# Turning diagonal blocks by DMA instead of by TensorE in a neighbour-skipping stage

## The chip, the cores and the metric

The kernel runs on one core of a Trainium2 chip. The metric is device time in microseconds: the median over runs of one execution of the whole kernel. Engines are named as in the profile: PE (TensorE, with PEld for its weight loads), DVE (VectorE), ACT (ScalarE), POOL (GpSimd) and SP (SyncE, which here issues DMAs only). A single profiled execution gives the trace that is read below.

## The reference, cut to what matters

There are 16 graphs of 1024 nodes with 128 features. Layer 0 is a gated graph network: four times, messages are gathered over the adjacency matrix and a GRU cell updates the node states. Layer 1 is a three-layer graph convolution on a thinned ("dilated") adjacency matrix. The thinning goes row by row over each matrix, and each row's removals also clear the matching column, so later rows see what earlier ones removed:

```python
row = jnp.take(carry, n, axis=0)
num = jnp.sum(row.astype(jnp.int32))
sf = jnp.where(num > T_DIL, (num + K_DIL - 1) // K_DIL, 1)
rank = jnp.cumsum(row.astype(jnp.int32))
rm = row & (rank % sf == 0)          # dropped where the mask and num > 1 allow
carry = carry.at[n].set(row & ~rm)
carry = carry.at[:, n].set(carry[:, n] & ~rm)
```

Layer 0 uses the full adjacency, and both layers end in a residual sum and a layer norm.

## The kernel before, in words

The first stage runs layer 0 (class `Gated`) and the thinning (class `FixPoint`) side by side. Everything after it (class `Sage`) is layer 1. The order of instructions on every engine, SP included, is the order in which the program writes them: the stage is scheduled by hand.

`Gated` keeps two graphs under way. A layer of one graph is, for PE, two passes of the message matmuls (L1092, a high and a low part) and then, for two halves, the gate matmuls (L1104) with turns of the other graph's state between them (L1037). Gate results lie in six PSUM banks that are used in rotation. DVE reads two of them per half (L1116, L1118), and PE can take a bank again only when its reader is done. POOL updates the state (L1123 to L1125) and issues the loads of the adjacency rows (h_a) and features (h_x).

`FixPoint` works through 32 blocks. A block is 128 rows (number k of 8) of four graphs (G = 4). It is written as a generator, `steps`; `Gated` advances it by one `yield` at each of its `aside` calls, about two layers to a block. A block holds four tiles f_a of 128 x 1024 bf16, which POOL's DMAs load (L687) about one block ahead. Its work: TensorE turns the diagonal 128 x 128 block of each f_a into PSUM tile f_pd (L770); DVE multiplies it with the untransposed one (L777), which tells which pairs of new rows are joined both ways, and POOL keeps the part above the diagonal (L778). DVE drops what earlier blocks removed (`keep`, L729) and takes running sums along the rows (`count`, L737). Then come three rounds of a fixed-point iteration on the diagonal block. The scan of `count` has a second operand that its second operation bypasses; it was the first column of the turned block's PSUM tile, broadcast.

The finished block's rows are made at the start of the next block (class `Block`): four times f_u on ACT (L910, L913), f_w (L864) and f_nr (L866) on DVE; SP stores f_nr (L867) and turns its next diagonal strip by DMA into f_rt (`read_last`, L723). Older strips of f_rt come back from DRAM, again turned by DMA (`read_back`, L716), in the middle of a block. Both kinds are DMA transposes on SP's queue.

A third job crosses the two: `load_test` (L994) loads 128 rows of adjacency into h_test from SP, and `check` (L1982) has DVE look whether all are 0 or 1. A load is written at the end of one layer and its check at the start of the next one:

```python
if n == 9 and s == 0:
    self.load_test(b0 // 2 * L0 + l)
if n == 1 and s == 1 and not checked:
    self.check(b0 // 2 * L0 + l)
```

There is one such pair per block. The tile has one buffer, so a load waits for the check before it.

Of the kernel before, what the change touches and what calls it, by code (L numbers as in the profile page):

```python
# [8 lines left out]
F32 = mybir.dt.float32  # L9
BF = mybir.dt.bfloat16  # L10
# [11 lines left out]
P = 128  # L22
B = 16
N = 1024
# [31 lines left out]
class Dilate:  # L56
# [15 lines left out]
    def __init__(self, ctx, tc, cst, adj, not_r):  # L72
        self.tc, self.nc, self.cst, self.adj, self.not_r = tc, tc.nc, cst, adj, not_r
        nc = self.nc
        pool = lambda name, **k: ctx.enter_context(tc.tile_pool(name=name, **k))
        self.one = pool("d_one", bufs=1)
        self.two = pool("d_two", bufs=2)
        self.small = pool("d_small", bufs=3)
        self.dram = pool("d_dram", bufs=1, space=DRAM)
        self.ps = pool("d_ps", bufs=1, space=PSUM)  # L80

        self.removed = [self.dram.tile([N, N], BF, name=f"rt{b}") for b in range(B)]

        self.coef = self.one.tile([B, ROW], F32, name="coef")  # L90
        nc.vector.memset(self.coef, 1.0)
        nc.vector.memset(self.coef[:, TAIL + 1:TAIL + 2], -1.0)
        nc.vector.memset(self.coef[:, TAIL + 2:TAIL + 3], -0.5)
        nc.vector.memset(self.coef[:, TAIL + 5:TAIL + 6], 2.0)
        self.stage = self.one.tile([P, B, ROW], BF, name="stage")
        for i, v in ((1, -8.5), (2, 1.0), (3, MAGIC), (4, -MAGIC), (5, 0.0)):
            nc.vector.memset(self.stage[:, :, TAIL + i:TAIL + i + 1], v)
        self.counts = self.one.tile([P, B, NB], F32, name="counts")
        self.free = {}
# [531 lines left out]
class FixPoint:  # L631
# [17 lines left out]
    G = 4  # L649
    LOTS = 8  # L650

    def __init__(self, ctx, tc, cst, adj, not_r, bad):
        self.tc, self.nc, self.cst, self.adj, self.not_r, self.bad = tc, tc.nc, cst, adj, not_r, bad
        nc, G = self.nc, self.G
        pool = lambda name, **k: ctx.enter_context(tc.tile_pool(name=name, **k))
        self.one = pool("f_one", bufs=1)
        self.two = pool("f_two", bufs=1)
        self.rows = pool("f_rows", bufs=self.LOTS)
        self.wide = pool("f_wide", bufs=3)
        self.rts = pool("f_rts", bufs=4)  # L660
        self.small = pool("f_small", bufs=2)
        self.ps = pool("f_ps", bufs=1, space=PSUM)

        tri = self.one.tile([P, P], F32, name="f_tri32")
        nc.vector.memset(tri, 1.0)
        nc.gpsimd.affine_select(tri, tri, pattern=[[1, P]], compare_op=ALU.is_ge, fill=0.0,
                                base=0, channel_multiplier=-1)
        self.tri = self.one.tile([P, P], BF, name="f_tri")
        nc.vector.tensor_copy(self.tri, tri)
        self.first = self.one.tile([P, NB, B], F32, name="f_first")  # L670
        nc.vector.tensor_scalar(self.first, cst["mask"], 0.0, -8192.0, op0=ALU.is_equal, op1=ALU.mult)


        self.tr = self.ps.tile([P, NB, P], BF, name="f_tr")
        self.sm = self.tr[:, NB - 1, :].bitcast(F32)[:, :12 * G].rearrange("p (a r g) -> p a r g", a=4, r=3)
        self.todo = [(k, b0) for b0 in range(0, B, G) for k in range(NB)]
        self.loaded = {}
        self.left = {}

    def load(self, c):  # L680

# [26 lines left out]
    def read_back(self, i, g):  # L708
# [5 lines left out]
        if k > 1:  # L714
            old = slice(0, (k - 1) * P)
            self.nc.sync.dma_start(rt[:, old], self.not_r[b0 + g, old, k * P:k * P + P], transpose=True)  # L716

    def read_last(self, i, g, nr):

        k = self.todo[i][0] + 1  # L720
        if k < NB:
            cols = slice((k - 1) * P, k * P)
            self.nc.sync.dma_start(self.left[i + 1, g][:, cols], nr[:, k * P:k * P + P], transpose=True)  # L723
# [5 lines left out]
            self.nc.vector.scalar_tensor_tensor(a[:, :k * P], rt[:, :k * P], 0.0, a[:, :k * P],  # L729
                                                op0=ALU.is_ge, op1=ALU.mult)  # L730

    def count(self, i, g, a, rank, other):
        nc = self.nc
        k, b0 = self.todo[i]
        out, start = rank[:, g, :], self.first[:, k, b0 + g:b0 + g + 1]

        nc.vector.tensor_tensor_scan(out, a, other[:, 0, 0:1].to_broadcast([P, N]), start,  # L737
                                     op0=ALU.add, op1=ALU.bypass)

    def steps(self):  # L740

        nc, G = self.nc, self.G
        for c in range(G):
            self.load(c)
        old = None
        for i, (k, b0) in enumerate(self.todo):
            diag = slice(k * P, k * P + P)

            yield
            if old:  # L750
                old.settle()
                old.wide_u(0)
            yield
            if old:
                old.wide_u(1)
                old.rows(0)
            yield
            if old:
                old.wide_u(2)
                old.rows(1)  # L760
            yield
            if old:
                old.rows(2)
                old.wide_u(3)
                old.rows(3)
            a = [self.loaded.pop((i, g)) for g in range(G)]
            pt = self.ps.tile([P, G, P], F32, name="f_pd")
            turned = pt.rearrange("p g n -> p (g n)").bitcast(BF)[:, :G * P].rearrange("p (g n) -> p g n", g=G)
            for g in range(G):
                nc.tensor.transpose(turned[:, g, :], a[g][:, diag], self.cst["ident_b"])  # L770
            yield
            if old:
                old.last_u()

            both = self.small.tile([P, G, P], BF, name="f_both")
            for g in range(G):
                nc.vector.tensor_mul(both[:, g, :], a[g][:, diag], turned[:, g, :])  # L777
            nc.gpsimd.affine_select(both, both, pattern=[[0, G], [1, P]], compare_op=ALU.is_gt, fill=0.0,  # L778
                                    base=0, channel_multiplier=-1)
            yield  # L780
            rank = self.two.tile([P, G, N], F16, name="f_rank")
            self.keep(i, 0, a[0])
            self.count(i, 0, a[0], rank, pt)
            yield
            yield
            self.keep(i, 1, a[1])
            yield
            self.count(i, 1, a[1], rank, pt)
            if i == 0:

                for c in range(G, self.LOTS):
                    self.load(c)
            yield
            yield
            yield
            self.keep(i, 2, a[2])
            self.count(i, 2, a[2], rank, pt)
            yield
            for g in range(G):
                self.read_back(i + 1, g)  # L800
            yield
            self.keep(i, 3, a[3])
            self.count(i, 3, a[3], rank, pt)

            num = self.sm[:, 0, 0, :]
            nc.vector.tensor_scalar(num, rank[:, :, N - 1], 1.0, None, op0=ALU.mult)
            q = self.params(num, 0)
            u = self.diag_u(rank[:, :, diag], q)
            if old:
                old.check()  # L810
                for g in range(G):
                    self.load(G * (i - 1) + g + self.LOTS)
            yield
            x = self.removed(u, q, both)
            yield
            yield
            pd, num = self.less(x, rank, 1)
            rd = self.small.tile([P, G, P], F16, name="f_rd")
            q = self.params(num, 1, lambda: nc.vector.tensor_sub(rd, rank[:, :, diag], pd))
            u = self.diag_u(rd, q)  # L820
            yield
            x = self.removed(u, q, both)
            yield
            old = self.Block(self, i, a, rank, both, x)
            yield
        yield
        old.settle()
        for n in range(4):
            old.wide_u(n)
            if n < 3:  # L830
                yield
            old.rows(n)
        yield
        old.last_u()
        yield
        old.check()
# [1231 lines left out]
```

## Time and profile before

| | |
|---|---|
| median of 3 runs | 2207.2 us (2204.59 to 2207.37) |
| profiled execution, its own time | 2207.94 us |
| its span, first to last instruction | 2206.2 us |
| busy: PE, DVE, ACT, POOL | 2099.8, 1836.0, 1327.2, 1233.9 us |
| transposes that go, L770 | 128, first at 33.5, last at 1224.0 us |
| scans, L737 | 128, 2345 ns each |
| DMA transposes on SP already there | 112 (L723) and 96 (L716) |
| h_test loads, L994 | 32, first issued at 1.3, last at 1231.5 us |

Layer 0 and the thinning fill the time from about 34 to 1260 us; loading and preparing of weights comes before, layer 1 after. A line of the timeline begins with start and length in microseconds, then engine ("q": of its sequencer), line, operation, output<-inputs, shape and count. A line of busy time per stretch begins with the stretch and its length; then follow busy time (and instructions) of PE, PEld, DVE, ACT and POOL, the granted PE clock, the share of the DMA engines that was busy, and GB/s. Of a DMA instruction, the length is the issue, not the transfer.

### The profile page before, as it was taken

How to read it: one execution, taken by the hardware profiler on the slowest of the kernel's cores; microseconds unless marked ns; L12 is line 12 of the kernel's file. 1: busy time of each engine (PE TensorE's matmuls, PEld its weight loads, DVE VectorE, ACT ScalarE, POOL GpSimd, SP SyncE). 2: the span in 40 equal slices, each digit the busy share in tenths (PEclk: the TensorE clock that was granted, in tenths of full speed). 3: DMA queues.
4: the chain of work that ended last, by engine and by line, in shares of the span. 5: the costliest groups of instructions: out<-in, count | busy, mean ns of one | idle time of the engine just before them, and what ended most of it. 6: DMA issues, size and time to landing. Idle time of an engine off the chain costs nothing. (4 is left out here: it accounts for less than half of the span.)

```text
span 2206.2 us, 32924 instructions
## 1 busy us (share of the span) xinstructions
PE 2099.8 (95%) x10217; PEld 1441.5 (65%) x10217; DVE 1836.0 (83%) x4213; ACT 1327.2 (60%) x3238; POOL 1233.9 (56%) x1218
## 2 busy tenths in 40 slices
PE   6999999999999999999999979999999899999987
PEld 4666556666666665666655657777777678887865
DVE  4898998889998889989889978888888666766877
ACT  3657466565656666465575656666666355555756
POOL 4458558567476475585575457777777255540002
PEclk9999999999999999999999989999999999999989
DMA  8247446366364394472584178888887577764404
GB/s 254 76 107 244 90 115 223 85 179 184 84 202 129 80 256 110 91 241 78 126 237 101 52 263 309 304 306 306 305 305 259 210 249 248 248 225 171 139 30 143
DMA packets 233853, 406.13 MB, mean 184 GB/s; under 512 B 79042, under 2 KB 100196, under 8 KB 233668
## 3 DMA queue, kind: packets, MB, share of 16 engines
q1 hardware_dynamic: 187844, 284.37, 39.4%
q0 software_dynamic: 41472, 117.46, 19.8%
q10 hardware_dynamic: 4352, 2.11, 0.4%
q8 instruction: 83, 1.36, 0.2%
q14 instruction: 102, 0.84, 0.1%
HBM read 313.48 MB, written 109.25 MB: 192 GB/s over the span
## 5 line engine op out<-in xcount | busy, mean ns | idle before, releaser
L1104 PE MATMUL h_g<-h_h,h_wh 128*128 128x512 f32 x768 | 396.1, 597 | 3.3 <-DVE h_r L1116 3.3
L1104 PE MATMUL h_g<-h_ms,h_wi 128*128 128x512 f32 x768 | 392.2, 592 | 0.0
L1123 POOL TENSOR_TENSOR h_zh<-h_r,h_h 128x512 f32<-128x512 f32 x126 | 174.2, 1382 | 257.2 <-ACT h_r L1119 254.0
L737 DVE TENSOR_TENSOR_SCAN f_rank<-f_a,f_first,f_pd 128x1024 f16<-128x1024 bf16 x128 | 299.4, 2345 | 4.2
L1092 PE MATMUL h_g<-h_a,h_hi 128*128 128x512 f32 x1024 | 278.7, 413 | 1.0 <-DMA h_a<-in_adj_dram 0.9
L1503 POOL CAST p_b<-p_at 128x512 uint8<-128x512 f32 x256 | 219.8, 881 | 84.7 <-DVE p_at L1495 52.7
L1104 PEld LDWEIGHTS h_g<-h_ms,h_wi 128*128 128x128 f32 x768 | 145.5, 190 | 184.3 <-issue 168.9
L1092 PE MATMUL h_g<-h_a,h_lo 128*128 128x512 f32 x1024 | 261.8, 392 | 0.0
L1092 PEld LDWEIGHTS h_g<-h_a,h_hi 128*128 128x128 f32 x1024 | 190.1, 188 | 61.7 <-issue 22.2
L1396 ACT ACTIVATE s_junk<-s_o 128x128 bf16<-128x128 f32 x384 | 114.0, 298 | 175.2 <-DVE s_o L1389 164.6
L1092 PEld LDWEIGHTS h_g<-h_a,h_lo 128*128 128x128 f32 x1024 | 189.8, 188 | 38.6 <-DVE h_lo L1030 0.4
L1104 PEld LDWEIGHTS h_g<-h_h,h_wh 128*128 128x128 f32 x768 | 133.3, 190 | 100.3 <-issue 72.7
L1125 POOL TENSOR_TENSOR h_h<-h_h,h_zh 128x512 f32<-128x512 f32 x126 | 179.9, 1428 | 9.9
L1119 ACT ACTIVATE h_r<-h_r,h_bi 128x512 f32<-128x512 f32 x128 | 92.4, 722 | 149.2 <-DVE h_r L1118 149.2
L1124 POOL TENSOR_TENSOR h_zh<-h_z,h_zh 128x512 f32<-128x512 f32 x126 | 162.1, 1287 | 9.9
L1095 ACT COPY h_ms<-h_g 128x512 f32<-128x512 f32 x128 | 73.8, 577 | 150.8 <-PE h_g L1092 150.6
L910 ACT ACTIVATE f_u<-f_rank,f_q 128x128 f16<-128x128 f16 (+7 forms) x128 | 110.6, 867 | 70.2 <-DVE f_rank L850 70.2
L1771 PE MATMUL q_ob<-s_wxp,q_xt 128*128 128x256 f32 x512 | 125.7, 390 | 0.3
L1982 DVE SCALAR_TENSOR_TENSOR p_junk<-p_a 128x1024 bf16<-128x1024 f32 x96 | 125.7, 1309 | 0.0
L1495 DVE SCALAR_TENSOR_TENSOR p_at<-p_nr,p_u 128x128 fp32r<-128x128 bf16 (+1 forms) x192 | 102.5, 543 | 19.4 <-ACT p_at L1487 12.6
L887 ACT ACTIVATE f_pd<-f_rank,f_q 128x128 f32<-128x128 f16 x128 | 59.1, 462 | 96.5 <-DVE f_q L701 93.4
L1413 POOL TENSOR_TENSOR q_rl<-s_r,q_rh 128x512 fp32r<-128x512 f32 x32 | 41.2, 1288 | 128.8 <-ACT q_rh L1412 105.8
(256 smaller groups left out, 4770.7 us busy)
## 6 DMA issues: line engine op xcount, KB each, us to landing
h_a<-in_adj_dram POOLq DMA_DIRECT2D x128, 512.0 KB, 9.2
p_a<-in_adj_dram SPq DMA_DIRECT2D x96, 512.0 KB
f_a<-in_adj_dram POOLq DMA_DIRECT2D x128, 256.0 KB, 6.5
e_nr<-f_nr SPq DMA_DIRECT2D x128, 256.0 KB
p_nr<-e_nr SPq DMA_DIRECT2D x32, 1024.0 KB
h_test<-in_adj_dram SPq DMA_DIRECT2D x32, 512.0 KB
s_at<-p_b SPq DMA_DIRECT2D x32, 512.0 KB
s_ag<-s_ag SPq DMA_DIRECT2D x64, 256.0 KB
```

The source lines that it names most:

```text
L737: nc.vector.tensor_tensor_scan(out, a, other[:, 0, 0:1].to_broadcast([P, N]), start, op0=ALU.add, op1=ALU.bypass)
L910: nc.scalar.activation(u[:, :n1], rank[:, g, :n1], AF.Abs, bias=q[:, 1, g:g + 1], scale=q[:, 0, g:g + 1])
L1092: nc.tensor.matmul(pm[f], part[:, j, :], st.adj[j][:, half[f]], start=(j == 0 and n == 0), stop=(j == NB - 1 and n == 1))
L1104: nc.tensor.matmul(pg, lhs, rhs, start=(i == 0), stop=(i == len(mm) - 1))
L1123: aid.tensor_tensor(d, r, h, ALU.subtract)
L1124: aid.tensor_tensor(d, z, d, ALU.mult)
L1125: aid.tensor_tensor(h, h, d, ALU.add)
L1396: self.nc.scalar.activation(junk, o[:, i, :], AF.Square, accum_out=ss[:, i:i + 1])
L1495: self.nc.vector.scalar_tensor_tensor(g["at"][:, j, c0:c0 + low], v[:, j, c0:c0 + low], 0.0, pu[:, :low], op0=ALU.is_lt, op1=ALU.is_lt)
L1503: self.nc.gpsimd.tensor_copy(g["b", f][:, j, :], g["at"][:, j, f * HF:(f + 1) * HF].bitcast(F32))
L1771: nc.tensor.matmul(pb[:, i], g["xt"][:, f, blk], self.wxp, start=(i % 2 == 0), stop=False)
L1982: nc.vector.scalar_tensor_tensor(junk, a, 0.0, a, op0=ALU.is_gt, op1=ALU.not_equal, accum_out=bad[:, c:c + 1])
```

## The change

The diagonal blocks of new rows are no longer turned by PE. A new function, `read_own`, issues one DMA transpose per graph from the f_a tile in SBUF into a new SBUF tile f_own. It is called for block 0 after its loads, and for block i + 1 at the end of block i. DVE's multiplication reads f_own. The scan's bypassed operand becomes a column of another PSUM tile (f_tr) that is set to zero once.

```diff
         self.sm = self.tr[:, NB - 1, :].bitcast(F32)[:, :12 * G].rearrange("p (a r g) -> p a r g", a=4, r=3)
+        self.none = self.sm[:, 1, 0, 0:1]
+        nc.vector.memset(self.none, 0.0)
...
+    def read_own(self, i):
+
+        if i >= len(self.todo):
+            return
+        k = self.todo[i][0]
+        t = self.own[i] = self.two.tile([P, self.G, P], BF, name="f_own")
+        for g in range(self.G):
+            self.nc.sync.dma_start(t[:, g, :], self.loaded[i, g][:, k * P:k * P + P], transpose=True)
...
-        nc.vector.tensor_tensor_scan(out, a, other[:, 0, 0:1].to_broadcast([P, N]), start,
+        nc.vector.tensor_tensor_scan(out, a, self.none.to_broadcast([P, N]), start,
                                      op0=ALU.add, op1=ALU.bypass)
...
         for c in range(G):
             self.load(c)
+        self.read_own(0)
...
-            pt = self.ps.tile([P, G, P], F32, name="f_pd")
-            turned = pt.rearrange("p g n -> p (g n)").bitcast(BF)[:, :G * P].rearrange("p (g n) -> p g n", g=G)
-            for g in range(G):
-                nc.tensor.transpose(turned[:, g, :], a[g][:, diag], self.cst["ident_b"])
+            turned = self.own.pop(i)
...
             x = self.removed(u, q, both)
             yield
+            self.read_own(i + 1)
             old = self.Block(self, i, a, rank, both, x)
             yield
```

More of the change, by code (lines that the diff above doesn't have):

```diff
@@ L675, in __init__ @@
         self.sm = self.tr[:, NB - 1, :].bitcast(F32)[:, :12 * G].rearrange("p (a r g) -> p a r g", a=4, r=3)
+        self.none = self.sm[:, 1, 0, 0:1]
+        nc.vector.memset(self.none, 0.0)
         self.todo = [(k, b0) for b0 in range(0, B, G) for k in range(NB)]
         self.loaded = {}
-        self.left = {}
+        self.left, self.own = {}, {}
     def load(self, c):
@@ L730, in keep, with count @@
                                                 op0=ALU.is_ge, op1=ALU.mult)
-    def count(self, i, g, a, rank, other):
+    def count(self, i, g, a, rank):
         nc = self.nc
@@ L782, in steps @@
             self.keep(i, 0, a[0])
-            self.count(i, 0, a[0], rank, pt)
+            self.count(i, 0, a[0], rank)
             yield
@@ L787, in steps @@
             yield
-            self.count(i, 1, a[1], rank, pt)
+            self.count(i, 1, a[1], rank)
             if i == 0:
@@ L796, in steps @@
             self.keep(i, 2, a[2])
-            self.count(i, 2, a[2], rank, pt)
+            self.count(i, 2, a[2], rank)
             yield
@@ L802, in steps @@
             self.keep(i, 3, a[3])
-            self.count(i, 3, a[3], rank, pt)
+            self.count(i, 3, a[3], rank)
             num = self.sm[:, 0, 0, :]
```

## The prediction

> **What bounds the kernel now.** I read the page, then busy time per stretch, then TensorE's own order, then what stands on SP's queue. The change lies in the first stage, from 34 to 1260 us; the busy time of that one stretch is
>
> ```profile
> 34.00:1260.00 1226.00, 1216.27 (x4548) 743.07 (x4548) 1091.48 (x2261) 746.80 (x1392) 756.78 (x732) 1.00 0.52 142
> ```
>
> PE is busy 1216 of 1226 us, DVE 1091 (89%). The ends of matmuls are modelled, so I checked PE's starts against the smallest pitch of each kind: they run like clockwork: beside a fixed 0.4 us where L1092 follows L1104, I find some 14 us of stalls in the stage. PE sets the end; DVE has 11% to spare but is tied closely to it. The timeline of PE around one group of the transposes that go:
>
> ```profile
> 679.29 1.99 PE L1092 MATMUL h_g<-h_a,h_lo 128*128 128x512 f32 x8
> 681.12 0.40 PE L770 MATMUL f_pd<-ident_b,f_a 128*128 128x128 bf16 x4
> 681.35 1.08 PE L1104 MATMUL h_g<-h_h,h_wh 128*128 128x512 f32 x2
> ...
> 688.71 0.60 PE L1037 MATMUL h_g<-ident,h_h 128*128 128x128 f32 x4
> 689.15 1.02 PE L1104 MATMUL h_g<-h_h,h_wh 128*128 128x512 f32 x2
> ```
>
> Four transposes hold PE from 681.12 to 681.35. Next the timeline of SP (columns: start, length):
>
> ```profile
> 642.07 3.70 SPq L867 DMA_DIRECT2D e_nr<-f_nr  x4
> 645.87 0.61 SPq L994 DMA_DIRECT2D h_test<-in_adj_dram  x1
> 682.52 0.33 SPq L867 DMA_DIRECT2D e_nr<-f_nr  x1
> 682.91 1.11 SPq L723 DMA_TRANSPOSE f_rt<-f_nr  x1
> ```
>
> SP issues in order and is idle for most of a block, so h_test, which DVE checks at 678.16, is issued at 645.87, far ahead of need. Then DVE from that check on:
>
> ```profile
> 678.16 1.22 DVE L1982 SCALAR_TENSOR_TENSOR h_junk<-h_test 128x1024 bf16<-128x1024 f32 x1
> 679.30 0.08 DVE L1982 DVE_READ_ACCUMULATOR h_junk<-h_test 128x1 f32 x1
> 679.45 1.37 DVE L864 TENSOR_SCALAR f_w<-f_u,f_q 128x1024 bf16<-128x1024 f16 x1
> 680.85 1.65 DVE L866 TENSOR_TENSOR f_nr<-f_w,f_a 128x1024 bf16<-128x1024 bf16 x1
> 682.42 1.49 DVE L864 TENSOR_SCALAR f_w<-f_u,f_q 128x1024 bf16<-128x1024 f16 x1
> 683.94 0.69 DVE L866 TENSOR_TENSOR f_nr<-f_w,f_a 128x1024 bf16<-128x1024 bf16 x1
> ...
> 686.80 0.60 DVE L777 TENSOR_TENSOR f_both<-f_a,f_pd 128x128 bf16<-128x128 bf16 x4
> 687.33 0.74 DVE L1116 SCALAR_TENSOR_TENSOR h_r<-h_g,h_bh,h_r 128x512 f32<-128x512 f32 x1
> ```
>
> There is no gap from the check to L1116, whose end (688.07) frees a bank that PE takes at 689.15: 1.08 us of slack. Last, the four f_a loads of the next block, issued by POOL from 666.38 to 668.67 (the tile view of f_a in that window):
>
> ```profile
> DMA to landing us min/median/max: 8.2/9.3/9.7
> ```
>
> The last lands at 668.67 + 9.7 = 678.3, after the check has begun.
>
> **What the Trainium skill says.** "VectorE: DVE Perf Modes", The three transpose paths: 390 ns for a 128x128 bf16 transpose on TensorE, 1309 ns by DMA. Here the pitch on PE is far less, 56 to 60 ns, and SP is held 1107 ns by each transpose of this shape (L723); the data of one issued at 603.44 had moved by 604.86, 1.4 us. "SBUF — State Buffer", Who interferes with whom: DVE and GpSimd share a port pair, and whichever comes second blocks. The trace agrees: L864 takes 0.48 us alone and 1.37 or 1.49 while POOL runs L1123 to L1125 (679.10 to 683.6). "DMA: Bandwidth & Descriptors", Queues, rings and completion order: each DMA engine takes the queues in turn. The trace shows transfers of several queues at once at 10 to 26 us.
>
> **The change part by part.**
>
> PE transposes. From the last L1092 before the group to the L1104 after it is 0.464 us; without a group it is 0.228. So 0.236 us per group. The first group lies in the start, 31 in the stage: 7.3 us. In seven blocks (below) PE will wait for DVE anyway and the saving only lengthens that wait: 24 x 0.236 = 5.7 us gained.
>
> DVE's L777 reads SBUF instead of PSUM: 213 ns each, 0.53 us per four. Not shown by the trace: no gain at worst, half (0.27 us) at best; taken as 0.1. Hidden, since DVE isn't the bound, except in the seven blocks, where it is below a microsecond in all.
>
> The scan's operand stays an f32 column in PSUM; 2345 ns each as before. Its memset comes once, before anything waits for DVE. Nothing for both. POOL's f_a loads get one more wait, on transposes of a block earlier: nothing, unless those were a block late.
>
> 128 new DMA transposes on SP: 4.4 us of SP per block, 142 us in all, where SP idles some 20 us per block. Each moves 32 KB as some 123 packets of 256 B that take 2.7 us of one DMA engine, 0.17 us of all 16. They land before L777 wants them: the last is issued at about 678.4 and L777 stands at 686.80. The transfers are hidden. Their place on SP is not.
>
> **What stands behind them.** In the built order of the changed program each block has on SP: four read-backs, the four new transposes of the next block, h_test, then stores and read_last. So h_test cannot be issued before the next block's four f_a tiles have landed and been turned. Before, it waited for neither. DVE waits for h_test at L1982, and behind that stand four f_w/f_nr pairs, L777 and L1116, for which PE waits.
>
> How late is it? Last f_a landing (L), against the check (C), in the block in each four where POOL issues f_a behind h_x and h_a of a new graph: L 212.82, 368.39, 522.99, 678.34, 833.12, 990.46, 1144.26; C 211.20, 367.88, 521.81, 678.16, 831.90, 989.30, 1143.11. L-C sums to 7.0 us over seven. To each I add 0.5 (three earlier transposes share saturated DMA engines with f_a), 1.2 (the fourth transpose on SP, 1.11 and its issue) and 3.6 (from h_test's issue to its data and semaphore: an undisturbed one, issued at 609.91, is through at 613.23, 3.3 us, plus a little for e_sum, issued at 678.48). DVE's wait is then 7.0 + 7 x 5.3 = 44.1 us over seven, 6.3 each.
>
> How much reaches PE? While DVE waits, POOL finishes its three operations, so DVE afterwards runs at its undisturbed lengths: 1.29 + 4 x 1.12 + 0.53 + 0.74 = 7.0 us from check to the end of L1116, taken as 7.1. In the old trace PE takes the bank 10.98 us after the check (10.96 to 10.99 in all seven). Cover: 3.88 us each. PE loses 44.1 - 7 x 3.88 = 16.9 us, 2.4 a time.
>
> In the other 25 blocks f_a lands early (in the block checked at 638.63 by 628.57): h_test arrives 1.5 to 5 us ahead of the check, nearest in the first block and where read-backs delayed it already (old landing 1099.5 against a check at 1103.16). Nothing, but thin; and they have some cover behind.
>
> Start. h_test was the second DMA, issued at 1.27, and 512 KB moved until 4.6 us while the weights were being loaded. It now comes after the start. The weights get what it used: 0.5 MB at the 266 GB/s of that stretch is 1.9 us. The last weights landed at about 28 and PE's work runs from there to 33.7 without another long wait, so I take 2 us gained (0 to 2.5). The first four own transposes wait for weights too, until some 28, and are needed at 34: hidden.
>
> Sum against the profiled execution (span 2206.2, time 2207.94, so 1.7 around it): 2206.2 - 5.7 - 2.0 + 16.9 = 2215.4 span, 2217.1 time. The median of the runs is 0.7 below that execution: 2216.4, so 2216.5.
>
> **The rivals.**
> 1. The wait does not reach PE: faster. The place is DVE's L1982; the price is the 3.88 us of cover, and the sign turns when DVE's wait falls below 3.88 + (5.7 + 2.0)/7 = 5.0 us each. If it stays under 3.88, all of 7.3 + 2 is kept: 2207.2 - 9.3 = 2198. For it: f_a could land earlier, once the old h_test no longer competes with the loads. Against: L alone is past C in all seven, and 1.2 + 3.3 follow in series.
> 2. The cover fails: POOL and DVE collide again later, ACT's f_u comes late, or read-backs make other blocks late too. With only the 0.8 us of bank slack (1.08 in the block shown), PE loses 44.1 - 5.6 = 38.5: 2207.2 - 7.7 + 38.5 = 2238. For it: thin margins elsewhere. Against: POOL's three operations depend on nothing behind the check.
> 3. It cancels: waits at the low end (3.3 instead of 3.6, no 0.5) give 44.1 - 5.6 - 27.2 = 11.3; with the gains 2207.2 - 9.3 + 11.3 = 2209, which a measurement can't tell from no change.
>
> **How the numbers follow.** A difference under about 0.2% (4.4 us) is not told from none here. Forecast case 0.62 (own range 2208 to 2226, 0.11 of it under 2211.6), rival 1 0.10, rival 2 0.18, rival 3 0.10. Faster 0.10, same 0.21, slower 0.69. The range runs from the edge of rival 1 to most of rival 2: 2203 to 2235.
>
> **What would show it.** L770 gone from PE; L1037 to L1104 waits for DVE L1116 of 2 to 3 us at seven places some 155 us apart; DVE idle before L1982 on the h_test DMA, about 44 us in all, in just those seven; L994 issued about 1.2 us after the last f_a lands; L864 and L866 undisturbed after it; PE's first L1092 about 2 us earlier. I am wrong if L1982 shows no idle time, if many other blocks wait too, or if the start does not move.

## The result, and the profile after

The changed kernel takes 2217.59 us (median of 5 runs, 2216.59 to 2218.07), the kernel before 2204.59 beside it (2201.55 to 2207.37): the ratio is 1.0057, with an interval of 1.0042 to 1.0071. It is about 0.6% slower, by 13.0 us. The profiled execution of it has a span of 2215.8 us and a time of 2217.59. Of the 9.6 us between the two profiled spans, the start took 0.9 more (first message matmul at 34.61 instead of 33.73), the first stage 14.9 more (the distance from there to the start of the last gate matmul is 1254.77 us instead of 1239.87), and layer 1 6.2 less.

The stretch from 34 to 1260 us no longer holds the same work, since the first stage now ends at 1290 us and ended at 1274. So here is the whole first stage of each, from the first message matmul to the last gate matmul, the kernel before first:

```profile
33.73:1274.20 1240.47, 1230.74 (x4598) 751.14 (x4596) 1104.21 (x2283) 758.54 (x1413) 762.27 (x736) 1.00 0.52 143
34.61:1289.97 1255.36, 1229.92 (x4473) 750.53 (x4472) 1088.57 (x2285) 758.13 (x1413) 758.57 (x735) 0.99 0.55 143
```

PE is busy 1229.9 us where it was 1230.7: it lost the transposes, but some of its matmuls take longer, as is seen below. Its idle time went from 9.7 to 25.4 us. DVE is busy 15.6 us less. The tile view of h_test tells where DVE idles:

```profile
L1004 SPq DMA_DIRECT2D h_test<-in_adj_dram x32: 571/578/1562, 48.0 to 1247.3; - x32
...
its engine sat idle before it (us, times) until:
  DMA h_test<-in_adj_dram: 33.5, 7
```

Seven waits, at the seven blocks that were named, of 3.3 to 6.7 us. The one that was shown of the kernel before is a typical one. First SP's timeline of the changed kernel, then DVE's, then PE's:

```profile
649.21 3.71 SPq L877 DMA_DIRECT2D e_nr<-f_nr  x4
681.08 5.49 SPq L727 DMA_TRANSPOSE f_own<-f_a  x4
686.62 0.58 SPq L1004 DMA_DIRECT2D h_test<-in_adj_dram  x1
```

```profile
690.58 1.23 DVE L1992 SCALAR_TENSOR_TENSOR h_junk<-h_test 128x1024 bf16<-128x1024 f32 x1 [5.47 <-DMA h_test<-in_adj_dram]
691.73 0.08 DVE L1992 DVE_READ_ACCUMULATOR h_junk<-h_test 128x1 f32 x1
691.73 0.48 DVE L874 TENSOR_SCALAR f_w<-f_u,f_q 128x1024 bf16<-128x1024 f16 x1
692.25 0.69 DVE L876 TENSOR_TENSOR f_nr<-f_w,f_a 128x1024 bf16<-128x1024 bf16 x1
...
696.23 0.62 DVE L786 TENSOR_TENSOR f_both<-f_a,f_own 128x128 bf16<-128x128 bf16 x4
696.77 0.74 DVE L1126 SCALAR_TENSOR_TENSOR h_r<-h_g,h_bh,h_r 128x512 f32<-128x512 f32 x1
```

```profile
695.29 0.60 PE L1047 MATMUL h_g<-ident,h_h 128*128 128x128 f32 x4
697.57 1.13 PE L1114 MATMUL h_g<-h_h,h_wh 128*128 128x512 f32 x2 [1.68 <-DVE h_r L1126]
```

h_test goes out at 686.62, where it went out at 645.87, and DVE idles 5.47 us for it. L874 and L876 then run at 0.48 and 0.69 us, undisturbed. From the check to the end of L1126 it is 6.93 us, and only 1.68 us of the 5.47 reach PE. The page has these waits on the costliest group of the kernel (columns after the bar: busy, mean ns, idle before it and its releaser). First before, then after:

```profile
L1104 PE MATMUL h_g<-h_h,h_wh 128*128 128x512 f32 x768 | 396.1, 597 | 3.3 <-DVE h_r L1116 3.3
L1114 PE MATMUL h_g<-h_h,h_wh 128*128 128x512 f32 x768 | 398.4, 600 | 10.8 <-DVE h_r L1126 10.8
```

So much was foreseen. Two more groups of PE idle longer, and these were not. First the kernel before, then the changed one (groups of the whole execution):

```profile
L1037 PE MATMUL h_g<-ident,h_h 128*128 128x128 f32 x512 | 77.3, 274 | 9.2 <-DVE h_h L1125 4.9 <-ACT h_r L1113 4.3
L902 PE MATMUL f_pd<-f_tri,f_x 128*128 128x128 bf16 x256 | 25.0, 220 | 1.1 <-DVE f_x L894 1.1
```

```profile
L1047 PE MATMUL h_g<-ident,h_h 128*128 128x128 f32 x512 | 77.7, 275 | 12.0 <-ACT h_r L1123 7.2 <-DVE h_h L1135 4.9
L912 PE MATMUL f_pd<-f_tri,f_x 128*128 128x128 bf16 x256 | 25.0, 220 | 7.2 <-DVE f_x L904 7.2
```

L1047 (L1037 before) waits longer for ACT, 7.2 instead of 4.3 us. L912 (L902 before) waits for DVE's f_x at four places of the stage. Before, PE idled 0.3 us at each; now 2.2 us at three of them and 0.6 at the fourth. This is PE at the first:

```profile
203.20 0.38 PE L912 MATMUL f_pd<-f_tri,f_x 128*128 128x128 bf16 x4 [2.21 <-DVE f_x L904]
203.42 0.61 PE L1047 MATMUL h_g<-ident,h_h 128*128 128x128 f32 x4
203.86 1.55 PE L1114 MATMUL h_g<-h_h,h_wh 128*128 128x512 f32 x2
205.21 1.91 PE L1114 MATMUL h_g<-h_ms,h_wi 128*128 128x512 f32 x2
```

Two gate matmuls that take 1.02 us elsewhere take 1.91 after the stall. From here on, a stall before L912 is counted from start to start beyond the usual 0.43 us: 0.4 us at each place before, now 2.37, 2.40, 2.40 and 0.71. Where does the delay in DVE's f_x come from? The waits of DVE name one more transfer (columns: total, times, longest); before, the second line was 7.4 us, 4 times, 2.3 at most:

```profile
DVE h_junk L1992 <- DMA h_test<-in_adj_dram: 33.5, 7, 6.7
...
DVE f_a L740 <- DMA f_rt<-f_nr: 10.9, 6, 3.5
```

### The profile page after: what moved, and what is told of

Same layout as the page of the kernel before. It is cut to its first block, busy times and chain, and to the rows that moved or that the text cites. A ratio compares the mean times of both kernels' runs of the same rounds, so it can differ in the third digit from the quotient of the medians.

```text
span 2215.8 us, 33030 instructions
## 1 busy us (share of the span) xinstructions
PE 2095.8 (95%) x10089; PEld 1437.7 (65%) x10089; DVE 1820.6 (82%) x4214; ACT 1326.3 (60%) x3238; POOL 1229.3 (55%) x1218
## 5 line engine op out<-in xcount | busy, mean ns | idle before, releaser
L748 DVE TENSOR_TENSOR_SCAN f_rank<-f_a,f_first,f_tr 128x1024 f16<-128x1024 bf16 x128 | 299.4, 2345 | 4.3
L787 POOL TENSOR_SCALAR_AFFINE_SELECT f_both<-f_both 128x512 bf16<-128x512 bf16 x32 | 20.5, 639 | 189.5 <-DVE f_both L786 189.5
```

Of the source, the lines that this page charges most:

```text
L748: nc.vector.tensor_tensor_scan(out, a, self.none.to_broadcast([P, N]), start, op0=ALU.add, op1=ALU.bypass)
```

## The experiments

Theory: SP's order is what costs. The own transposes wait for f_a, h_test stands behind them, DVE waits for h_test and PE for DVE. Rivals: the own transposes cost as transfers or as time of SP wherever they stand; or the loss comes from the late f_rt strips alone. In all there are two switches, PE's transposes (kept or gone) and the own transposes (none, ahead of h_test, or behind it), and the runs fill all six cells.

**h_test ahead of the own transposes.** Against the changed kernel:

```diff
             first = n == 7 and before not in (0, L0)
+            if n == 9 and s == 0:
+                self.load_test(b0 // 2 * L0 + l)
             if not first and n not in ("rest", 8):
                 next(steps, None)
             for job in jobs.get(n, ()):
                 job()
-            if n == 9 and s == 0:
-                self.load_test(b0 // 2 * L0 + l)
```

> The changed kernel with two things on SP's queue swapped: each block's h_test load is written ahead of the four own transposes instead of behind them; everything else is the same. In the trace of the changed kernel I count two kinds of new PE stalls in the first stage: behind DVE's seven waits for h_test (33.5 us on DVE, about 10.9 us on PE with the slow matmuls that follow one of them), and at about 203, 517, 831 and 1147 us, where DVE waits for an f_rt strip turned from f_nr (about 6.2 us on PE above what was there before, and 5.0 us of matmuls at double pitch behind three of them). Theory (head of line, for both: h_test at the same time crowds the queue of the strips only if it is late): the seven waits go to 0, and the time falls by 10.9 us at least, to 2206.7, and to 2195.5 if the second kind goes too. Rival (the second kind comes from the own transposes themselves): the second kind stays, 2206 to 2207. Rival (the transfers of the own transposes slow everything whatever their order): within 4 us of the changed kernel, 2214 to 2218.

Measured: 2201.76 us, ratio to the kernel before 0.9974 (0.9962 to 0.9987). SP's timeline, at the place shown above:

```profile
641.04 3.71 SPq L877 DMA_DIRECT2D e_nr<-f_nr  x4
644.80 0.73 SPq L1004 DMA_DIRECT2D h_test<-in_adj_dram  x1
673.10 5.79 SPq L727 DMA_TRANSPOSE f_own<-f_a  x4
```

No wait for h_test is left. The own transposes are all there and still stand ahead of the stores and strips of the next block. The same instructions in another order turn a loss of 0.6% into a gain of 0.26%. The rival that blames the transfers falls. The second kind of stall did not go: one of the four places still stalls 2.40 us, and the others 0.71 or 0.72 instead of 0.4.

**The own transposes added to the kernel before.** PE still turns the blocks and nobody reads f_own:

```diff
...
+        self.read_own(0)
         old = None
...
+            self.read_own(i + 1)
             old = self.Block(self, i, a, rank, both, x)
```

> The kernel before with the 128 own transposes added at the changed kernel's place on SP, into a tile that nobody reads; PE still turns the blocks and DVE and the scan read those. It prices the transposes on SP's queue alone. Theory: all that was lost comes from there: the seven waits for h_test and the late strips, 10.9 + 11.2 = 22.1 us, and 0.9 in the start: 2204.6 + 23 = 2227.6, or about 3 us less since layer 1 ran that much shorter in the changed kernel. Rival (the loss needs f_own as DVE's operand, or the missing PE transposes): 2204 to 2212.

Measured: 2220.45 us, 1.0055 (1.0041 to 1.0069). The view of h_test:

```profile
  DMA h_test<-in_adj_dram: 42.7, 8
```

The whole loss is there without the change's other half, but not the 22 to 23 us that I had expected: the late strips hardly came along (one stall of 2.07 us before the same matmul, three of 0.4), and the waits for h_test are longer than in the first trace of the changed kernel. It looks as if the two were coupled: what holds up DVE ahead of the check leaves less of a wait for h_test. The ledger below returns to it.

**The same, behind h_test.**

```diff
             first = n == 7 and before not in (0, L0)
+            if n == 9 and s == 0:
+                self.load_test(b0 // 2 * L0 + l)
...
-            if n == 9 and s == 0:
-                self.load_test(b0 // 2 * L0 + l)
```

> The kernel before with the 128 own transposes added into a tile that nobody reads, as in the run of 2220.5 us, but written behind the h_test load of their block instead of ahead of it. PE still turns the blocks. Theory (the place on SP's queue is everything): no wait for h_test, 2206.6 as the kernel before, within 2 us. Rival (the own transposes' 4.4 us of SP a block and their transfers cost as such): 2210 to 2220.

Measured: 2207.90 us, 1.0004 (0.9994 to 1.0014), no wait for h_test. Its first stage takes 1239.81 us where it took 1239.87. 128 DMA transposes, 149 us of SP, cost nothing that can be measured when they stand behind h_test; the interval of the whole time leaves room for 3 us.

**PE's transposes alone, by the block itself.** DVE multiplies the block with itself, no own transposes:

```diff
-        self.read_own(0)
...
-            turned = self.own.pop(i)
+            turned = [t[:, diag] for t in a]
...
-                nc.vector.tensor_mul(both[:, g, :], a[g][:, diag], turned[:, g, :])
+                nc.vector.tensor_mul(both[:, g, :], a[g][:, diag], turned[g])
...
-            self.read_own(i + 1)
```

> The changed kernel without its 128 own transposes: DVE multiplies the diagonal block with itself instead of with the turned one, so the turning is left out altogether and the removals are other ones; shapes and instruction counts are otherwise those of the changed kernel. It prices PE's 128 transposes alone against the kernel before. Theory: 31 groups of 0.236 us on the path, 7.3 us: 2204.6 - 7.3 = 2197.3, no wait for h_test, stalls at 203, 517 and 831 us back at 0.4 us, the start as before. Rival (the groups fill gaps that PE has anyway): 2203 to 2206.

This missed: 8144.1 us, since the thinning did not settle; its trace goes on with a long second thinning that no other run has. Its first stage lies ahead of that (1235.15 us), and led to the next expectation.

**PE's transposes alone, by zeros.** A tile of zeros in place of the turned block:

```diff
...
-        self.read_own(0)
...
-            turned = self.own.pop(i)
+            turned = self.zero
...
-            self.read_own(i + 1)
```

> The changed kernel without its own transposes, and nothing turned in their place: DVE multiplies the diagonal blocks with a tile of zeros, so pairs of new rows joined both ways are left out of the thinning; in the run that multiplied with the block itself the thinning did not settle and a repair of about 5.9 ms followed, here nothing can be unsettled. It gives the price of PE's 128 transposes in the whole time. By that other run's first stage (first message matmul to last gate 1235.2 us against 1239.9 before): theory, 4.7 us less than before, 2201.9. Rival (my count of 24 to 31 groups of 0.236 us): 5.7 to 7.3 less, 2199 to 2201.

Measured: 2204.68 us, 0.9993 (0.9982 to 1.0003). Neither 4.7 nor 7.3 us came; it can't be told from no gain. Its trace has no own transposes and no wait for h_test, but the 2.4 us stalls before L912 at two of the four places. So the own transposes are not needed for them. That was against what I had thought. Why this kernel is 3 to 4 us behind the one with h_test first, which has the own transposes besides, is not settled: it has one long stall more in its trace, and it thins differently, so its layer 1 isn't comparable.

**The changed kernel again.**

> The changed kernel once more, for a second trace. In the first trace four stalls of PE (203, 517, 831, 1147 us) follow a strip f_rt that lands late. Theory A (the late check and the own transposes make the strips late each time): again 2.4 us at three or four of those places, and half-pitch matmuls behind them. Theory B (a strip that is half a microsecond later tips a DVE operation into POOL's port time, and the transfers of the own transposes only make that more likely): at other places or fewer, 0.7 or 2.4 us and nothing between. In both, seven waits for h_test, 30 to 45 us in all, and a median of 2215 to 2219.

Measured: 2217.49 us, 1.0052 (1.0039 to 1.0065). Seven waits for h_test, 40.5 us. Stalls before L912 of 0.72, 0.71, 2.40 and 0.72 us, where the first trace had 2.37, 2.40, 2.40 and 0.71. This is theory B: the stall differs from execution to execution, and takes two values. The traces of all kernels agree: of the sixteen places in the four traces of kernels that kept PE's transposes and the written order of stores, fifteen stall 0.4 us and one 2.07; of the 28 places in the seven such traces without PE's transposes, all stall either 0.7 or 2.4.

**Which strip?** In the kernel with h_test first, the place that stalls (511.54) is preceded by this on DVE, and by this on POOL:

```profile
499.83 2.23 DVE L740 SCALAR_TENSOR_TENSOR f_a<-f_rt,f_a 128x512 bf16<-128x512 bf16 x1 [0.57 <-DMA f_rt<-f_nr]
```

```profile
500.20 1.30 POOL L1133 TENSOR_TENSOR h_zh<-h_r,h_h 128x512 f32<-128x512 f32 x1
501.59 1.61 POOL L1134 TENSOR_TENSOR h_zh<-h_z,h_zh 128x512 f32<-128x512 f32 x1
```

The strip held L740 back by 0.57 us, into the time in which POOL updates the state, and L740 took 2.23 us instead of some 0.7. The Trainium skill ("SBUF — State Buffer", Who interferes with whom) says that DVE and GpSimd share a port pair under an exclusive lock. The trace fits in that L740 is slow where it overlaps POOL's operations, but it doesn't show who held the ports, and no run here moved POOL's work. In all the traces the two go together: every stall of 2.07 us or more has such an L740, of 1.6 to 2.3 us, 11 to 12 us ahead of it, and at every place with a shorter stall that L740 takes 0.66 to 0.70 us. Where it waited 0.19 to 0.42 us for its strip it stayed short, and where it waited 0.49 to 0.96 us it became long; four long ones follow a longer wait of an earlier L740 instead.

If the strip is the cause, an earlier strip must cure it. Against the kernel with h_test first, the strip's transpose goes ahead of the row's store on SP:

```diff
-            nc.sync.dma_start(fix.not_r[self.b0 + g, self.k * P:(self.k + 1) * P, :], nr)
             fix.read_last(self.i, g, nr)
+            nc.sync.dma_start(fix.not_r[self.b0 + g, self.k * P:(self.k + 1) * P, :], nr)
```

> The kernel with h_test ahead of the own transposes (2201.8), and besides, in each finished row the transpose that turns the diagonal strip (f_rt) is written on SP ahead of the store of that row instead of behind it. Theory (the stalls of PE before L912 at four places come from strips that land late behind stores in the same queue, and without PE's transposes POOL's gate update comes 0.3 us earlier and meets the late DVE operation): DVE's waits for f_rt fall from 9.3 us to under 5, the four stalls fall to 0.7 us at most with none of 2.4, and the time by 2 to 5 us, to 2197 to 2200. Rival (the strips are late because the adjacency loads fill the DMA engines, whatever the order on SP): waits for f_rt 7 us or more, 2200 to 2203.

Measured: 2200.15 us, 0.9968 (0.9956 to 0.9981). DVE's waits for f_rt, which were 9.3 us, and PE at the place of the stall:

```profile
DVE f_a L740 <- DMA f_rt<-f_nr: 1.2, 4, 0.4
```

```profile
510.93 0.38 PE L912 MATMUL f_pd<-f_tri,f_x 128*128 128x128 bf16 x4 [0.34 <-DVE f_x L904]
```

No 2.4 us stall is left; the four are 0.50 to 0.54, below the 0.71 that was the least in every trace without PE's transposes. So the strip's place does set the stall. That the long value is gone for good is not shown by one trace: the run that multiplied the block with itself had none either, without this edit. And the first stage is no shorter than in the trace without it (4.2 us below the kernel before in both; the ledger below shows where the gain goes). The time is the lowest ratio of all, but its interval overlaps that of the kernel without this edit, so the 2 to 5 us are not shown. Its control, the same edit in the kernel before:

> The kernel before with the strip's transpose written ahead of the store of its row, and nothing else. Theory: DVE's waits for f_rt fall from 7.4 us to under 4, the four stalls of 0.4 us go, 1.7 us at most: 2204.7. Rival: no change, 2206.4.

Measured: 2206.25 us, 1.0000 (0.9990 to 1.0011). The waits for f_rt fell to 0.2 us and the L902 stalls to 0.25 at most, and PE had so little to gain (1.0 us) that the time does not show it.

**h_test first, again.**

> The kernel with h_test ahead of the own transposes once more, beside the other two, for a second trace and a second interval. Theory: 0.9974 of the kernel before again, within 0.001 either way, no wait for h_test, and stalls before L912 of 0.7 or 2.4 us at the four places (where each falls may differ).

Measured: 2200.88 us, 0.9978 (0.9965 to 0.9990), no wait for h_test, stalls of 0.72, 0.72, 2.41 and 0.73. In the first trace of this kernel the long one was another of the four.

**The start.** h_test first, and its very first load at the start of the program:

```diff
         self.load_weights()
+        self.load_test(0)
         next(steps)
...
-            if n == 9 and s == 0:
+            if n == 9 and s == 0 and b0 + l:
```

> As the kernel with the h_test load ahead of the own transposes (2201.8), and the very first h_test load goes out at the start of the program again, ahead of the first own transposes, as it did in the kernel before. It tells what the start owes to h_test. Theory (the own transposes and their wait make the start later, h_test costs nothing there): within 1 us, 2201 to 2203, first message matmul at 33.5 to 34.5. Rival (my step of the prediction: h_test's 512 KB in the start cost 2 us): 2203.8, first message matmul about 2 us later, 36.

Measured: 2199.98 us, 0.9975 (0.9966 to 0.9984), first message matmul at 33.94 where the same kernel without the edit had 34.03 and 33.52. An h_test load at the start costs nothing that these traces show.

**The scan's operand.** The kernel before with the one new operand:

```diff
-        nc.vector.tensor_tensor_scan(out, a, other[:, 0, 0:1].to_broadcast([P, N]), start,
+        nc.vector.tensor_tensor_scan(out, a, self.none.to_broadcast([P, N]), start,
```

> The kernel before with the scan's bypassed operand moved to the zeroed column of f_tr, and nothing else of the change. Theory: nothing, scans 2345 ns each, 2202 to 2207. Rival (the scan no longer waits for the turned block and its PSUM buffer comes free earlier): up to 2 us faster, 2202.6.

Measured: 2205.39 us, 0.9997 (0.9989 to 1.0005). Nothing, as said.

The six cells, medians in us (the kernel before was 2204.6 to 2206.6 beside them):

| | no own transposes | behind h_test | ahead of h_test |
|---|---|---|---|
| PE transposes kept | 2204.6 to 2206.6 (before) | 2207.9 | 2220.5 |
| PE transposes gone | 2204.7 (zeros) | 2201.8, 2200.9 | 2217.6, 2217.5 (the change) |

The place on SP's queue is worth 13 to 17 us; PE's transposes 3 to 7 where the own ones are there, and some 2, which can't be told from nothing, where they aren't.

## Why the prediction came out as it did

The first stage as a ledger: apart from the transposes that went, PE's matmuls run in one fixed order, so the difference in time can be added up from the distances between starts. Each entry is the sum of those distances minus the same sum of the kernel before, us:

| | changed | again | own added | h_test first | strip first |
|---|---|---|---|---|---|
| groups of L770, with what follows them | -7.3 | -7.3 | 0.0 | -7.3 | -7.3 |
| gate matmuls that follow a turn (DVE late from h_test) | +8.4 | +14.0 | +13.7 | +0.2 | +0.6 |
| L912 after a gate matmul (DVE late from a strip) | +6.2 | +2.8 | +1.6 | +2.8 | +0.4 |
| L1047 after a gate matmul (ACT not done) | +3.4 | +2.0 | -0.1 | +2.7 | +3.3 |
| gate matmul after gate matmul (pitch) | +5.2 | +1.8 | +3.8 | -2.1 | -1.8 |
| rest | -0.9 | -2.1 | -1.7 | -0.6 | +0.7 |
| first stage | +14.9 | +11.2 | +17.3 | -4.2 | -4.2 |

**The head of the line: right, in mechanism and places.** Exactly the seven named blocks wait, and no other in either trace of the changed kernel. The transfers of the own transposes are hidden and their place is not: the six cells show it.

**The length of the wait: right parts, one term too large and two too small.** For the seven I had 44.1 us; the traces have 33.5 and 40.5 (41.4 with the PE transposes kept, leaving out an eighth wait of 1.3). By terms: from the last f_a landing to h_test's issue I took 8.4 us (7 x 1.2) and it is 9.7 and 9.5; from issue to check 25.2 (7 x 3.6), and it is 29.9 in both. What failed is L-C: 10.5 with the half microseconds for the earlier transposes, against -6.0 and +1.0. The check comes later than I took it to, above all behind the three stalls at L912 of the first trace: there f_a landed 2.1 to 2.7 us before DVE was ready for the check.

**The cover: right.** 3.88 us a block were said. In the second trace 40.5 us of waits became 14.0 on PE, (40.5 - 14.0) / 7 = 3.8; with the own transposes added, (41.4 - 13.7) / 7 = 4.0. In the first trace three waits of 3.3 to 3.9 us cost PE 0.2 in all. So rival 1 was right about those three blocks and wrong about the other four. Rival 2, that the cover fails, fell.

**PE's transposes: the price right, the gain too large.** The groups' 7.3 us are gone to the tenth. But PE does not arrive alone at what comes next: 2.0 to 3.4 us return at L1047, where PE waits for the bank that ACT's sigmoid (L1123) reads, and at L912 1.2 to 6.2 (0.4 with the strip first). With every wait for h_test gone, 4.2 us of the 7.3 stay (3.6 in its second trace). I had left out the savings in seven blocks, and should have asked in all 31 what the next wait is. The wait at L1047 grew by 1.8 to 3.4 us in all eight traces without PE's transposes and by 0.3 at most in the others, so it goes with them.

**Missed: the strips and the clock.** I said of the other 25 blocks that nothing would happen. Four of them have a wait of DVE for f_rt that was in the old trace (7.4 us, 4 times), and PE idled 0.3 us at each of them. I saw it and did not ask how far it was from a collision with POOL. It costs 0.3 to 2.0 us more a place. The matmuls at double pitch behind long stalls, 5.2 us in the first trace, were in no step: they are the clock, as the last section shows.

**The start: wrong in sign.** I had 2 us gained from the weights. They do come earlier, the last 0.7 us (27.46 instead of 28.16). But PE idled 2.4 us before it, and the eight matmuls at L991 took longer. Before, then after:

```profile
29.65 3.24 PE L981 MATMUL h_g<-h_wi,h_w 128*128 128x384 f32 x8
```

```profile
29.06 4.98 PE L991 MATMUL h_g<-h_wi,h_w 128*128 128x384 f32 x8
```

Their starts are 0.64 us apart, where most of them were 0.32 apart before. The record of the granted clock explains that: its first entry, of the full clock, stands at 33.56 us, where it stood at 30.64 before. In all 13 traces the starts are 0.64 apart until that entry, at 29.87 to 33.56 us, and 0.32 after it. So the eight matmuls became 1.7 us longer, which outweighs the earlier weights: I had taken the work from the weights to the first message matmul as fixed, and it is not. The first message matmul comes 0.9 us later here; it lies at 33.5 to 35.0 us in the eight traces with own transposes and at 33.0 to 33.7 in the five without. Why the full clock tends to come later with them is not settled. The run with the early h_test load shows no gain from keeping h_test out of the start.

**The operand of L777, the scan, SP's own time: right.** L786 takes 218 ns a piece, L777 took 213; I had taken a small gain, and there is a loss of 5 ns, hidden.

**The sum: luck.** 2215.4 was said of the span, and 2215.8 came. That is closer than the steps deserve. Against the kernel before I had said 9.3 us more. Said: -5.7 - 2.0 + 16.9. In the trace: groups -7.3, start +0.9, h_test +8.4, L912 +6.2, L1047 +3.4, pitch +5.2, rest -0.9, and layer 1 -6.2. The last is no effect of the change: layer 1 lies between 926.3 and 933.0 us in the traces of all kernels that thin alike, 932.6 in the one of before and 926.4 and 926.6 in the two of the change, but also 926.3 and 930.0 in the two of h_test first. With layer 1 as before, the span would have been 2222. The medians, which do not depend on one trace, differ by 13.0 and 11.1. The size of the steps that were foreseen, 9.2 together, was nearly right only because the waits for h_test, which I took to cost PE 3 to 8.5 us more than they did, stood for others that I had not seen.

## What to carry to other kernels

On a queue that issues in order, as SP's does here, a new instruction can cost nothing by its own length and a lot by what it waits for: list what stands behind it, when that was issued before, and put what has waited for nothing so far ahead of it. Here two statements in the other order are the difference between 0.6% slower and 0.26% faster. A saving on the engine that sets the end is not in hand until the next wait of that engine is known: of 7.3 us, some 4 stayed. And a sum that comes out right should still be taken apart, since several of its terms here were wrong.

## What the runs showed of the hardware

- After some PE stalls the fp32 gate matmuls run at 0.855 us instead of 0.429, for about 3.4 us, and the granted clock falls to half (0.53 on average from 1013.0 to 1016.5 in the first trace of the changed kernel, where its record has 3.41 us at 0.5). The Trainium skill ("TensorE: Matmul & The Clock Gate", What's actually happening) has a clock that goes to half after an idle activity window of about 3.4 us, and a window that does not restart with the kernel. The length fits, and a free-running window would explain why only some stalls are followed by it: in the first stages of all traces no stall with less than 2.3 us from start to start was, and of 17 that were longer, 9 were. Each costs up to 1.7 us more. The page's rule of thumb (Why this matters for your kernels), no idle gap above some 3 us, is too generous here.
- A DVE operation with both operands in SBUF was not faster than with one in PSUM, at 128x128 bf16: 218 against 213 ns. The Trainium skill ("VectorE: DVE Perf Modes", The perf-mode tier table) puts bf16 in SBUF at twice the rate of any PSUM operand for long rows; at this size nothing of it is seen.
- 0.57 us of lateness became 2 us of it: a DVE operation that slips into POOL's time took 2.23 us instead of about 0.7. So the stall behind it took one of two values, 0.7 or 2.4 us without PE's transposes and 0.4 or 2.07 with them, and none between, as long as the store came ahead of the strip.
- At the start, too, PE ran at double pitch until the first entry of the full clock, which came anywhere from 29.87 to 33.56 us in the 13 traces. A first message matmul that moves by a microsecond from one execution to the next need not come from the DMAs.
